# Layer 1's second pass with one matrix a channel and the pixels around the patches in pairs

## The chip, the cores and the metric

The kernel is one program on 1 core of a Trainium2 chip. The metric is the device time of one execution in microseconds (us). All arithmetic is in 32-bit floats. The core has TensorE (PE, matrix products out of the on-chip SBUF into the accumulators of PSUM), VectorE (DVE), ScalarE (ACT), GpSimd (POOL) and SyncE (SP), and 16 DMA engines that move data between HBM and SBUF. A transfer is begun by an instruction on SP, ACT or POOL.

## The reference

Four layers are applied, each with a residual, to `x` of 4 images x 48 channels x 256 x 256 pixels. The change is in layer 1, cut here to what matters:

```python
y = jnp.einsum('oc,bchw->bohw', w_in, x)              # 48 -> 288 channels
yp = y.reshape(B, C2, ht, P, wt, P).transpose(0, 1, 2, 4, 3, 5)
f = jnp.fft.rfft2(yp) * fft_mask[None]                 # in each 8 x 8 patch
yp = jnp.fft.irfft2(f, s=(P, P))
y = yp.transpose(0, 1, 2, 4, 3, 5).reshape(B, C2, H2, W2)
y = lax.conv_general_dilated(y, w_dw, ..., padding=((1, 1), (1, 1)), feature_group_count=C2)
x1, x2 = jnp.split(y, 2, axis=1)
g = jax.nn.gelu(x1, approximate=False) * x2            # 144 channels
return jnp.einsum('oc,bchw->bohw', w_out, g)
```

So for each of 288 channels: a filter within 8 x 8 patches, then a 3 x 3 convolution, which also needs pixels of the neighbouring patches; then the channels are multiplied in pairs.

## The kernel before

**Two streams.** `run` (L1210) emits two interleaved streams of work. Stream "a" runs layers 0 and 1 image by image, then layer 3 of all images; stream "b" runs the first statistics, `patch_weights`, and layer 2 of each image. Each generator yields a cost in a planner's units, and the stream whose clock is behind is advanced next (L1246). Afterwards a scheduler of the framework moves instructions on each engine by the times that it expects, except where `pinned` holds them. Layer 2 of image i is therefore executed beside layers 0 and 1 of image i+1; only image 0's layers 0 and 1 have no layer 2 beside them. `dma` (L213) begins transfers on SP for stream a and on POOL for stream b; layer 2's `look` (L890) begins its loads on ACT.

**Layer 1** has three stages for an image. The first pass (L616-636) makes the 288 channels and stores them to `hD` in HBM. The second pass (L637-715), which is what changes, applies filter, convolution and gate and stores to `gD`. The third stage (L716-770) projects back to 48 channels.

**Second pass.** A patch pair of 8 x 16 pixels is put on the 128 partitions, and the 512 patch pairs of the image are the columns. The 288 channels go in 72 groups (NG) of 4. For each group g, `fetch` (L678) begins four loads one group ahead: `hg` (1 MB, the pixels), `ct` (the filter, 128 x 128 a channel), `tt` (the nine taps as a 128 x 128 matrix from the pixels of the patch pair itself) and `ht` (the taps from the 52 pixels around it). Then for each channel

1. `filtered` (L652): a 128 x 128 matrix times 512 columns (L654), copied from PSUM to `ys`, by ACT for even channels (L660) and by DVE for odd ones (L658);
2. the rows of pixels around each patch pair are brought from `ys` to `yh` by 8 copies from SBUF to SBUF a group (L708-711): two of 16 rows, two of 8 rows, four of one row. They hold all four channels of the group, 2244 elements a row;
3. `gated` (L662), one group later (`todo`): the taps on the own pixels (L667, 128 rows) and on the pixels around (L668, 65 rows) are added up in one PSUM bank; for a pair of channels ACT applies gelu (L671) and DVE multiplies (L672) into `gt`. Every second group `gt` (1 MB) is stored to `gD` (L713).

That is 12 matrix products of 512 columns and 12 or 13 transfers a group. A 32-bit product is two instructions in the profile, so 1152 products are 2304 rows. Stream a has five PSUM banks.

**`patch_weights`** (L546) runs once, in stream b, beside layer 0 of image 0. A first loop over 72 groups makes the filter matrices by a product (L565) and stores them to `cD`; it yields 3 units a group. A second loop makes the tap matrices (L577) and stores them to `tD`; it yields 12 units for each of 15 blocks.

Of the kernel before, what the change touches and what calls it, by code (L numbers as in the profile page):

```python
# [8 lines left out]
F32 = mybir.dt.float32  # L9
I32 = mybir.dt.int32  # L10
AF = mybir.ActivationFunctionType
# [8 lines left out]
NS = 16  # L20
# [9 lines left out]
YW = 17  # L30
YC = 33 * YW
Y0 = YW + 1
YL = Y0 + 4 * YC + Y0


AROUND = [
# [2 lines left out]
]  # L39
NH = 52  # L40

NZ = 65

# [130 lines left out]
class Net:  # L176
# [369 lines left out]
    def patch_weights(self):  # L546


        nc, a = self.nc, self.a
        self.cD = self.dram.tile([NG, 128, 4, 128], F32, name="cD")[:]  # L550
        self.tD = self.dram.tile([4 * NG, (128 + NH) * 128], F32, name="tD")[:]
        with ExitStack() as ctx:
            w = ctx.enter_context(self.pool("pw", 1))
# [1 line left out]
            mask = self.filter_mask(a["L1_fft_mask"], [(0, 4 * NG)], w)  # L555
            dw = w.tile([9, 4 * NG], F32, name="dw")
            self.dma(dw[:], a["L1_w_dw"])
            for g in range(NG):
                m = sb.tile([128, 4, 128], F32, name="m", tag="m")
                for c in range(4):  # L560
                    nc.vector.tensor_scalar(
                        m[:, c, :], self.ri, mask[:, 4 * g + c : 4 * g + c + 1], None, ALU.mult
                    )
                ps = self.bank()
                nc.tensor.matmul(ps[:], self.ri, m[:].rearrange("p c k -> p (c k)"), start=True, stop=True)  # L565
                ct = sb.tile([128, 512], F32, name="ct", tag="ct")
                nc.scalar.copy(ct[:], ps[:])
                self.dma(self.cD[g].rearrange("p c k -> p (c k)"), ct[:])
                yield 3
            for q0 in range(0, (128 + NH) * 128, 4608):  # L570
                sh = sb.tile([9, 4608], F32, name="sh", tag="sh")
                self.dma(sh[:], a["c_shift"][:, q0 : q0 + 4608])
                for c0 in range(0, 4 * NG, 96):
                    tt = sb.tile([96, 4608], F32, name="tt", tag="tt")
                    for q in range(0, 4608, 512):
                        ps = self.bank()
                        nc.tensor.matmul(ps[:96, :], dw[:, c0 : c0 + 96], sh[:, q : q + 512], start=True, stop=True)  # L577
                        if q % 1024:
                            nc.vector.tensor_copy(tt[:, q : q + 512], ps[:96, :])
                        else:  # L580
                            nc.scalar.copy(tt[:, q : q + 512], ps[:96, :])
                    self.dma(self.tD[c0 : c0 + 96, q0 : q0 + 4608], tt[:])
                    yield 12

    def layer1(self, x, mr, y):
        nc, a = self.nc, self.a
# [50 lines left out]
        with ExitStack() as ctx:  # L637
            w = ctx.enter_context(self.pool("wb", 1))
            sb = ctx.enter_context(self.pool("bb", 2))
            ys = [w.tile([128, YL], F32, name=self.nm("ys")) for _ in range(2)]  # L640
            yhs = [w.tile([NZ, YL], F32, name=self.nm("yh")) for _ in range(2)]
            hts = [w.tile([NZ, 4, 128], F32, name=self.nm("ht")) for _ in range(3)]
            for t in ys + yhs + hts:
                nc.vector.memset(t[:], 0.0)

            pick = lambda t, k, c: t[:k, Y0 + YC * c : Y0 + YC * c + 32 * YW].rearrange(
                "p (h s b) -> p s h b", h=2, b=YW
            )[:, :, :, :16]
            order = lambda t: t.rearrange("p (s h b) -> p s h b", h=2, b=16)
            todo, gt = None, None  # L650

            def filtered(c):  # L652
                ps = self.bank()
                nc.tensor.matmul(  # L654
                    ps[:].rearrange("p (s n) -> p s n", n=32), ct[:, c, :], hg[:, :, c, :], start=True, stop=True
                )
                if c % 2:
                    nc.vector.tensor_copy(pick(yt, 128, c), order(ps[:]))  # L658
                else:
                    nc.scalar.copy(pick(yt, 128, c), order(ps[:]))  # L660

            def gated(c):  # L662
                go, yo, yho, to, ho = todo
                both = []
                for q in (c, c + 2):
                    ps = self.bank()
                    nc.tensor.matmul(order(ps[:]), to[:, q, :], pick(yo, 128, q), start=True, stop=False)  # L667
                    nc.tensor.matmul(order(ps[:]), ho[:, q, :], pick(yho, NZ, q), start=False, stop=True)  # L668
                    both.append(ps)
                gl = sb.tile([128, 512], F32, name="gl", tag="gl")  # L670
                nc.scalar.activation(gl[:], both[0][:], AF.Gelu)  # L671
                nc.vector.tensor_mul(  # L672
                    gt[:, :, 2 * (go % 2) + c, :], gl[:].rearrange("p (s n) -> p s n", n=32),
                    both[1][:].rearrange("p (s n) -> p s n", n=32),
                )


            def fetch(g):  # L678
                hg = sb.tile([128, NS, 4, 32], F32, name="hg", tag="hg")
                self.dma(hg[:].rearrange("p s c n -> p s (c n)"), hD[:, g])  # L680
                ct = sb.tile([128, 4, 128], F32, name="ct", tag="ct")
                self.dma(ct[:], self.cD[g])
                tt = sb.tile([128, 4, 128], F32, name="tt", tag="tt", bufs=3)
                ht = hts[g % 3]
                tv = self.tD[4 * g : 4 * g + 4].rearrange("c (k m) -> k c m", m=128)
                self.dma(tt[:], tv[:128])
                self.dma(ht[:NH], tv[128:])
                return hg, ct, tt, ht

            fetched = {0: fetch(0)}  # L690
            for g in range(NG + 1):
                if g < NG:
                    yt = ys[g % 2]
                    if g + 1 < NG:
                        fetched[g + 1] = fetch(g + 1)
                    hg, ct, tt, ht = fetched.pop(g)
                if todo is not None and todo[0] % 2 == 0:
                    gt = sb.tile([128, NS, 4, 32], F32, name="gt", tag="gt")
                for c in range(2):
                    if g < NG:  # L700
                        filtered(2 * c)
                        filtered(2 * c + 1)
                    if todo is not None:
                        gated(c)
                if g < NG:
                    yh = yhs[g % 2]
                    n = YL - 2 * Y0
                    for k, m, p0, dp, far in AROUND:  # L708
                        self.dma(
                            yh[k : k + m, Y0 : Y0 + n], yt[p0 : p0 + (m - 1) * dp + 1 : dp, Y0 + far : Y0 + far + n]  # L710
                        )
                if todo is not None and todo[0] % 2:
                    self.dma(gD[:, :, todo[0] // 2, :], gt[:].rearrange("p s c n -> p s (c n)"))  # L713
                todo = (g, yt, yh, tt, ht)
                yield 12
        st = self.stat.tile([CP, 129, 6], F32, name=self.nm("st"), tag="st" + self.stream, bufs=1)  # L716
        with ExitStack() as ctx:
# [586 lines left out]
```

## Time and profile before

| | us |
|---|---|
| runs (3): lowest, median, highest | 20766.17, 20775.92, 20789.14 |
| the profiled execution | 20767.55 |
| its span (first to last instruction) | 20765.8 |

| engine | busy us | share of the span |
|---|---|---|
| PE | 18830.0 | 91% |
| DVE | 10830.0 | 52% |
| POOL | 8656.1 | 42% |
| ACT | 5784.0 | 28% |

Where the second pass stands in the span, by the first and last start of its own-pixel products (L667):

| image | from us | to us | beside it |
|---|---|---|---|
| 0 | 2359.1 | 3240.5 | nothing of stream b |
| 1 | 6250.8 | 7393.6 | layer 2 of image 0 |
| 2 | 10412.9 | 11562.3 | layer 2 of image 1 |
| 3 | 14576.6 | 15720.9 | layer 2 of image 2 |

The costliest rows of the second pass, mean duration of one instruction (they overlap, so products that follow one another start closer together than this):

| row | count | busy us | mean ns |
|---|---|---|---|
| L654 PE `ps<-hg,ct` 128*128, 512 columns | 2304 | 1268.5 | 678 |
| L667 PE `ps<-ys,tt` 128*128, 512 columns | 2304 | 1183.1 | 635 |
| L668 PE `ps<-yh,ht` 65*128, 512 columns | 2304 | 1186.7 | 660 |
| L658 DVE COPY `ys<-ps` | 576 | 397.2 | 690 |
| L672 DVE `gt<-gl,ps` | 576 | 395.4 | 687 |
| L660 ACT COPY `ys<-ps` | 576 | 344.7 | 603 |
| L671 ACT ACTIVATE `gl<-ps` | 576 | 343.9 | 597 |

In a row, `128*128` are the rows and columns of the matrix that is held in PE, and `128x512 f32` the operand that streams through. The idle time beside a group and its releaser say what that engine waited for. A queue such as "SPq" is the engine's sequencer, which begins transfers.

### The profile page before, as it was taken

To read this page: it belongs to the slowest core of one execution; us is meant where nothing else is said; L and a number is where in the kernel's file an instruction comes from. 1 tells how busy PE (TensorE), PEld (TensorE's weight loads), DVE (VectorE), ACT (ScalarE), POOL (GpSimd) and SP (SyncE) were. 2 spreads that over 40 slices of the span, in tenths; PEclk is the share of its full clock that TensorE was granted. 3 is DMA by queue.
4 is the path that set the end of the run, shared out by engine and by line. 5 is a ranking of instruction groups with operands and counts; after the bars stand their busy time and mean duration, and the time that the engine had idled before them with its cause. 6 is when DMAs were issued, how large, how long until landed. Compare 5 with 4: busy or idle time off the path is not lost.

```text
span 20765.8 us, 232624 instructions
## 1 busy us (share of the span) xinstructions
PE 18830.0 (91%) x79032; PEld 11956.8 (58%) x79032; DVE 10830.0 (52%) x21947; ACT 5784.0 (28%) x12185; POOL 8656.1 (42%) x8899
## 2 busy tenths in 40 slices
PE   7998798999878889998788899987888999999999
PEld 4566335666543346665433466654334787878888
DVE  4544322477764544777645447776554255555511
ACT  2333312333331123333311233333112211111111
POOL 1000000177754511777545117775552066666600
PEclk9899799999968999999689999996888999999999
DMA  4623886555588975555889755558897566766633
GB/s 113 133 57 78 231 217 202 133 129 132 127 244 228 236 214 134 128 133 127 239 230 234 220 133 128 130 126 240 231 235 222 137 148 151 157 151 153 146 78 71
DMA packets 2494456, 3403.86 MB, mean 164 GB/s; under 512 B 595079, under 2 KB 2069631, under 8 KB 2382732
## 3 DMA queue, kind: packets, MB, share of 16 engines
q1 hardware_dynamic: 1906184, 2081.72, 38.4%
q0 software_dynamic: 452944, 1110.52, 21.5%
q10 hardware_dynamic: 134144, 196.73, 4.2%
q8 instruction: 635, 10.40, 0.2%
q14 instruction: 549, 4.49, 0.1%
HBM read 2450.46 MB, written 802.77 MB: 157 GB/s over the span
## 4 chain that ended last, share of the span: by engine, by line
PE 72%; DMA 14%; DVE 6%; POOL 4%; issue 2%; SPq 1%; ACT 1%; ACTq 0%; DVEq 0%; POOLq 0%
PE ps L353 22%; PE ps L361 5%; PE ps L876 5%; PE ps L654 4%; POOL V L974 3%; PE ps L668 3%; PE ps L667 3%; DMA ct<-cD 3%; PE ps L623 3%; PE ps L754 3%; PE ps L1120 2%; PE ps L901 2%; PE ps L811 2%; PE ps L505 2%; DMA A<-x 2%
## 5 line engine op out<-in xcount | busy, mean ns | idle before, releaser
L974 POOL DMA_INDIRECT V<-t,idx x8192 | 8240.8, 1006 | 4821.2 <-issue 2346.6
L353 PE MATMUL ps<-W,A 128*128 128x288 f32 (+1 forms) x24576 | 5566.1, 375 | 102.9 <-DMA A<-x 35.9
L353 PEld LDWEIGHTS ps<-W,A 128*128 128x128 f32 x24576 | 4295.0, 192 | 1252.3 <-issue 533.7
L214 POOL DMA_DIRECT2D X<-x x192 | 144.4, 756 | 4242.6 <-DMA x<-xt 3034.9
L987 DVE TENSOR_TENSOR V<-V 128x1536 f32<-128x1536 f32 (+3 forms) x2048 | 1845.3, 901 | 19.5
L985 DVE TENSOR_TENSOR V<-V,w 128x3072 f32<-128x3072 f32 x512 | 1713.6, 3347 | 33.2 <-DMA V<-t,idx 23.8
L654 PE MATMUL ps<-hg,ct 128*128 128x512 f32 x2304 | 1268.5, 678 | 394.7 <-DMA ct<-cD 275.0
L623 PE MATMUL ps<-win,xp 48*128 48x288 f32 x4096 | 1093.1, 622 | 515.8 <-DVE xp L610 237.6
L434 ACT COPY qkv<-ps 128x288 f32<-128x288 f32 x2048 | 763.7, 401 | 2681.8 <-PE ps L353 1180.0
L876 PE MATMUL ps<-A,W 128*96 128x512 f32 x3072 | 1483.5, 619 | 3.0 <-issue 3.0
L668 PE MATMUL ps<-yh,ht 65*128 65x512 f32 x2304 | 1186.7, 660 | 142.9 <-DMA yh<-ys 113.9
L361 PE MATMUL ps<-W,B 58*128 58x288 f32 (+1 forms) x8192 | 1271.0, 393 | 30.0 <-DMA B<-x 18.3
L457 DVE BATCH_NORM_STATS2 bs<-ps 128x6 f32<-128x96 f32 x2048 | 390.1, 252 | 1654.9 <-PE ps L455 1654.4
L1100 DVE TENSOR_TENSOR gp<-gl,ps 128x192 f32<-128x192 f32 x1024 | 354.4, 352 | 1716.6 <-ACT gl L1099 1706.0
L667 PE MATMUL ps<-ys,tt 128*128 128x512 f32 x2304 | 1183.1, 635 | 60.3 <-DVE ys L658 33.1
L623 PEld LDWEIGHTS ps<-win,xp 48*128 48x128 f32 x4096 | 686.5, 274 | 892.3 <-ACT hs L630 286.9
L654 PEld LDWEIGHTS ps<-hg,ct 128*128 128x128 f32 x2304 | 472.0, 212 | 1037.5 <-issue 928.6
L1099 ACT ACTIVATE gl<-ps 128x192 f32<-128x192 f32 x1024 | 331.3, 330 | 2619.7 <-PE ps L353 2318.5
L672 DVE TENSOR_TENSOR gt<-gl,ps 128x512 f32<-128x512 f32 x576 | 395.4, 687 | 1236.8 <-PE ps L668 1236.2
L361 PEld LDWEIGHTS ps<-W,B 58*128 58x128 f32 x8192 | 764.8, 187 | 452.1 <-issue 353.4
L876 PEld LDWEIGHTS ps<-A,W 128*96 128x96 f32 x3072 | 487.2, 168 | 853.4 <-issue 839.6
L658 DVE COPY ys<-ps 128x512 f32<-128x512 f32 x576 | 397.2, 690 | 1086.0 <-PE ps L654 897.3
(182 smaller groups left out, 24329.4 us busy)
## 6 DMA issues: line engine op xcount, KB each, us to landing
hD<-hs SPq DMA_DIRECT2D x64, 4608.0 KB
hg<-hD SPq DMA_DIRECT2D x288, 1024.0 KB
gD<-gt SPq DMA_DIRECT2D x144, 1024.0 KB
gs<-gD SPq DMA_DIRECT2D x64, 2304.0 KB
V<-t,idx POOLq DMA_INDIRECT x8192
A<-x SPq DMA_DIRECT2D x512, 193.5 KB
xt<-x SPq DMA_DIRECT2D x256, 387.0 KB
A<-x ACTq DMA_DIRECT2D x512, 193.5 KB
```

The source lines that it names most:

```text
L353: nc.tensor.matmul(to(q, b), A[:, r + q, 128 * b + g : 128 * b + g + 128], W[:, g, :], start=b == 0 and g == 0, stop=b == 1 and g == 2,)
L361: nc.tensor.matmul(to(q, b), B[p, r // 2, 128 * b : 128 * b + 128], W[p, 3, :], start=b == 1, stop=b == 0)
L434: nc.scalar.copy(t.qkv[:, 2 * q + b, :], banks[2 * b + q][:, 0:288])
L623: nc.tensor.matmul(ps[:, :288], xp[64 * h : 64 * h + 48, b, :], win[64 * h : 64 * h + 48], start=True, stop=True,)
L654: nc.tensor.matmul(ps[:].rearrange("p (s n) -> p s n", n=32), ct[:, c, :], hg[:, :, c, :], start=True, stop=True)
L667: nc.tensor.matmul(order(ps[:]), to[:, q, :], pick(yo, 128, q), start=True, stop=False)
L668: nc.tensor.matmul(order(ps[:]), ho[:, q, :], pick(yho, NZ, q), start=False, stop=True)
L754: nc.tensor.matmul(pp[:CP, :], pr[:, q, :], got[q][:], start=q == 0, stop=q == 2)
L876: m = nc.tensor.matmul(to[q], W[:, g, :], A[:, q:4:2, g : g + 256], start=q == 0 and g == 0, stop=q == 1 and g == 2,)
L974: nc.gpsimd.indirect_dma_start(out=V[:, k, 4 * cr : 4 * cr + 4, :].rearrange("p e c -> p (e c)"), out_offset=None, in_=table, in_offset=ba ...
L985: self.pinned(nc.vector.tensor_mul(Vm, Vm, wm.unsqueeze(2).to_broadcast([128, 64, 48])))
L987: nc.vector.tensor_add(V[:, :, 0:n, :], V[:, :, 0:n, :], V[:, :, n : 2 * n, :])
```

## The change

**Tables.** `cD` is replaced by `fD`, one block of 128 x 4 x 192 numbers a group. Its first 128 columns a channel are the product of the filter and the nine taps on the own pixels; its last 64 are the 52 columns of the filter that make the pixels around, already in the order of `yh` (the rest is zero). `patch_weights` makes the taps `tD` first and then, for each group, loads the own taps back, makes the filter as before, copies 52 of its columns in eight pieces, multiplies filter and taps in four products of 128 columns, copies the result and stores the block. It yields 5 units a group, not 3.

**Second pass.** `filtered` is gone. `around` makes only the rows around: for channels c and c+2 two products with 64-column matrices that write partitions 0-63 and 64-127 of one PSUM bank, and one ACT copy to `ye`. `gated` makes the own part straight from `hg` with the composed matrix, all four products first, then the four products on the pixels around, whose rows lie at 0-51 and 64-115. Each of the eight copies `ye` to `yh` is now made twice, for the two halves of the partitions, with two channels (1122 elements) a row: one begun on SP, one on ACT. `ht` is loaded in two transfers, `ct` and `tt` in one (`f`); loads go two groups ahead, with four buffers.

```diff
-YL = Y0 + 4 * YC + Y0
+YL = Y0 + 2 * YC + Y0
...
-NZ = 65
+NF = 128 + 64
...
-            for g in range(NG):
-                m = sb.tile([128, 4, 128], F32, name="m", tag="m")
...
-                self.dma(self.cD[g].rearrange("p c k -> p (c k)"), ct[:])
-                yield 3
...
+            fs = [w.tile([128, 4, NF], F32, name=self.nm("f")) for _ in range(2)]
+            for f in fs:
+                nc.vector.memset(f[:], 0.0)
+            for g in range(NG):
+                own = sb.tile([128, 4, 128], F32, name="own", tag="own")
+                self.dma(own[:], self.tD[4 * g : 4 * g + 4].rearrange("c (k m) -> k c m", m=128)[:128])
...
+                f = fs[g % 2]
+                for k, n, p0, dp, far in AROUND:
+                    nc.vector.tensor_copy(
+                        f[:, :, 128 + k : 128 + k + n], ct[:, :, p0 : p0 + (n - 1) * dp + 1 : dp]
+                    )
+                ps = self.bank()
+                for c in range(4):
+                    nc.tensor.matmul(
+                        ps[:, 128 * c : 128 * c + 128], ct[:, c, :], own[:, c, :], start=True, stop=True
+                    )
+                nc.scalar.copy(f[:, :, 0:128], ps[:].rearrange("p (c k) -> p c k", k=128))
+                self.dma(self.fD[g], f[:].rearrange("p c k -> p (c k)"))
+                yield 5
...
+            def around(c):
                 ps = self.bank()
+                for q in range(2):
+                    nc.tensor.matmul(
+                        strips(ps[64 * q : 64 * q + 64, :]), f[:, c + 2 * q, 128:NF], hg[:, :, c + 2 * q, :],
+                        start=True, stop=True,
+                    )
+                nc.scalar.copy(pick(ye, slice(0, 128), c), order(ps[:]))
+
+            def gated():
+                go, hgo, fo, yho, ho = todo
                 both = []
+                for c in range(2):
+                    both.append([self.bank() for _ in range(2)])
+                    for q in range(2):
+                        nc.tensor.matmul(
+                            strips(both[c][q][:]), fo[:, c + 2 * q, 0:128], hgo[:, :, c + 2 * q, :],
+                            start=True, stop=False,
+                        )
+                for c in range(2):
+                    for q in range(2):
+                        rows = slice(64 * q, 64 * q + NH)
+                        nc.tensor.matmul(
+                            order(both[c][q][:]), ho[rows, c, :], pick(yho, rows, c), start=False, stop=True
+                        )
...
             def fetch(g):
+                hg = sb.tile([128, NS, 4, 32], F32, name="hg", tag="hg", bufs=4)
                 self.dma(hg[:].rearrange("p s c n -> p s (c n)"), hD[:, g])
+                f = sb.tile([128, 4, NF], F32, name="f", tag="f", bufs=4)
+                self.dma(f[:].rearrange("p c k -> p (c k)"), self.fD[g])
+                ht = hts[g % 4]
+                for q in range(2):
+                    self.dma(
+                        ht[64 * q : 64 * q + NH],
+                        self.tD[4 * g + 2 * q : 4 * g + 2 * q + 2].rearrange("c (k m) -> k c m", m=128)[128:],
+                    )
+                return hg, f, ht
...
+            fetched = {0: fetch(0), 1: fetch(1)}
             for g in range(NG + 1):
                 if g < NG:
+                    ye, yh = yes[g % 2], yhs[g % 2]
+                    if g + 2 < NG:
+                        fetched[g + 2] = fetch(g + 2)
+                    hg, f, ht = fetched.pop(g)
+                    for c in range(2):
+                        around(c)
+                if todo is not None:
...
+                    gated()
                 if g < NG:
                     n = YL - 2 * Y0
                     for k, m, p0, dp, far in AROUND:
+                        for q, dma in ((0, self.dma), (64, nc.scalar.dma_start)):
+                            dma(yh[q + k : q + k + m, Y0 : Y0 + n], ye[q + k : q + k + m, Y0 + far : Y0 + far + n])
```

## The prediction

> **What bounds it now.** I read the page first, for where PE is not full, then busy time by stretch around the second pass, then who waited there for PE and for SP's queue, then the timeline of one group.
>
> ```profile
> PE   7998798999878889998788899987888999999999
> DMA  4623886555588975555889755558897566766633
> ```
> PE is near full except in four dips; DMA is high just there. The dips are layer 1. By stretch:
> ```profile
> 2346.00:3250.00 904.00, 829.91 (x1728) 345.24 (x1728) 207.98 (x296) 173.92 (x289) 0.00 (x0) 0.92 0.79 213
> 6234.00:7403.00 1169.00, 1016.95 (x2336) 430.23 (x2336) 605.14 (x892) 193.90 (x320) 612.06 (x639) 0.89 0.91 232
> ```
> (length, then busy PE, PEld, DVE, ACT, POOL; clock, DMA share, GB/s.) The second pass takes 904 us in image 0 and 1169 in image 1, 1180 and 1173 in images 2 and 3, PE busy 92% and 87%. From first to last start of L667 a group takes 881/71 = 12.4 us in image 0 and 1143/71 = 16.1 in image 1. PE isn't alone: the transfers are busy 91% there. SP's queue, image 1's stretch:
> ```profile
> SPq L214 <- DMA tt<-tD: 105.4, 46, 7.3
> SPq L214 <- DMA yh<-ys: 84.6, 70, 10.0
> SPq L214 <- DVE ys L658: 76.0, 40, 7.6
> SPq L214 <- DMA A<-x: 71.2, 20, 7.8
> ```
> (total us, times, longest.) SP issues for 660 us of this stretch, by the durations of its begins, and most of the rest it waits. It does not need `tt` or layer 2's `A` for anything. The instruction records say why it waits: every transfer begun by SP or ACT signals one of **eight semaphores**, in rotation over both queues, and its begin waits until the transfer eight places earlier has landed. So eight are in flight at most, and a late one stops whichever queue comes to its semaphore. One group:
> ```profile
> 2606.10 5.87 SPq L214 DMA_DIRECT2D yh<-ys  x8
> 2606.93 3.73 PE L668 MATMUL ps<-yh,ht 65*128 65x512 f32 x8
> 2610.49 1.88 PE L654 MATMUL ps<-hg,ct 128*128 128x512 f32 x4
> 2612.08 0.60 SPq L214 DMA_DIRECT2D gD<-gt  x1
> 2612.77 1.95 SPq L214 DMA_DIRECT2D hg<-hD  x1
> ```
> SP issues eight copies for 5.87 us, then a store, then the next loads: no gap. Eight rows of PE take 2610.49 - 2606.93 = 3.56 us, 0.445 each, so 24 rows a group are 10.7 us.
>
> **PE, parts removed.** Filter, own and around were 24 rows. The own part stays: 8 rows, 3.56 us. The pixels around now stand on 52 rows in two halves of the array. The trace has such pairs in layer 0:
> ```profile
> 1500.47 3.08 PE L353 MATMUL ps<-W,A 128*128 128x288 f32 x12
> 1503.47 1.24 PE L361 MATMUL ps<-W,B 58*128 58x288 f32 x8
> 1504.64 3.18 PE L353 MATMUL ps<-W,A 128*128 128x288 f32 x12
> ```
> 12 full rows take 3.00 us (0.25 each), 8 paired rows 1.17 (0.146): 0.585 of the price, switching included. So the halo costs 8 x 0.445 x 0.585 = 2.08 us. `around` pairs columns, not rows, which no row here shows: 2.08 if it pairs like L361, 3.56 if not at all. I take 2.08. Sum 7.7 us a group (9.2), 3.0 (1.5) less.
> The Trainium skill (TensorEngine Tiling (Array Packing), Tiling Modes) says that column tiles work independently, like row tiles; by it the lower price holds, and no run here shows it yet.
>
> **Other engines.** DVE loses two copies a group (0.690 each), ACT keeps two copies and two gelus (0.60 each). Both have room: DVE 605 of 1169.
>
> **Transfers, bytes.** From the packet records in image 0's stretch: `tt` 36864 packets of 512 B at 30 ns and `ct` 9216 of 2 KB at 86 go, 69 + 50 us over 16 engines; `f` is 9216 of 3 KB, at `ct`'s rate 129 ns, 74 us. The copies move the same bytes (3456 packets of 8976 B, 878 ns, become 6912 of half). Work 711 (0.787 x 904) - 45 = 666 us; in image 1, 1060 - 45 = 1015.
>
> **Transfers, begins.** This is the other side. SP has as many as before: 4 loads (two for `ht`), 8 copies, half a store: 650 us in image 0, 9.0 a group. ACT gets 8 copies, 2 x 0.59 + 2 x 0.61 + 4 x 0.73 = 5.3 us a group at SP's prices, in front of or between its copies and gelus. Through the eight semaphores go 20.5 transfers a group, not 12.5. Time from begin to landing, from the begins and the increments of the semaphores (fastest tenth and mean, image 0): `hg` 4.85 and 6.74; `ht` 5.87 and 7.68; an 8-row copy 4.29 and 6.81; a single row 2.33 and 4.18.
> The order is hg, f, ht, ht, then SP's and ACT's copies by turns. The third pair waits for `hg` and `f`, the fourth for the two `ht`, the eighth for the fourth. So from the begin of `hg`: `ht` begins at 1.4 (0.5 + 0.43 + 0.45) and lands at 7.3 to 9.1, the fourth copy then lands at 11.6 to 15.9, the eighth is issued (0.74), half a store (0.3): 12.6 to 16.9 us until the next `hg`. Half-sized packets save 0.4. Middle: 14.3. The same count for before (eighth copy waits for `ht`, nothing follows): 8.2 to 10.1, under PE's 10.7. **The rotation takes PE's place as the bound.** Image 0: 72 x (14.3 - 12.4) = +137.
> Image 1 (`ht` 6.24 and 8.71, 8-row 4.57 and 7.74): 13.2 to 18.9, middle 16.05 - 0.4 = 15.65, against 16.1 now. But SP's place in the rotation now depends on ACT's queue: layer 2's 154 ACT transfers a stretch (2.1 a group) cost SP 71.2/72 = 1.0 us a group; eight more cost between 0 and 8/2.1 x 1.0 = 3.8. I take the middle, 1.9: 17.55, 72 x 1.45 = +104 an image, +313 for three.
> Two loads in front do not help this: `hg` waited for its turn on SP, not for a buffer.
> The Trainium skill (DMA: Bandwidth & Descriptors, Rules for kernel authors) speaks against the split: two transfers to disjoint halves of the partitions share the same engines, one transfer is better; by it the copies gain nothing in bytes and pay twice the begins, as in my sum. Its page on SBUF (SBUF — State Buffer, Door 1) gives the halves different ports; if copies then ran at the 4608-byte gathers' 300 ns, 63 us less in image 0.
>
> **Tables.** `patch_weights` runs beside layer 0 of image 0, where PE is 97% busy (1570 of 1615 us), so its PE time is on the path. New: 8 rows of 128 columns a group. Lower price 0.153 (L811, 64 rows in 9.79 us), upper 0.25 (L353 with 288); I take 0.19, the length of a weight load: 72 x 8 x 0.19 = 109 us (88 to 144). Once it waits for the last `tD` to land, about 7. Its ACT copy (72 x 0.6), eight DVE pieces (72 x 8 x 0.17 = 98 us) and 0.4 MB more a group hide in engines under half busy there. The planner's 144 units more end long before layer 1 asks. +116.
>
> **Sum.** 20765.8 + 137 + 313 + 116 = 21,332; that execution took 20767.55 and the median is 20775.92, 8 us more, within the runs' own 23. I say **21,330**. Its own range, from the fast ends (12.2 us in image 0; 15.65 in the others; 95 for tables) to the slow ones, most of it: 20,950 to 21,700.
>
> **Rivals.**
> *Faster.* Small copies land early, the rotation never stops, and bytes bound the pass. For: 45 us less work, PE down by a quarter, no more waits of L654 for `ct`. Against: 20.5 x mean landing. Image 0 at 90% DMA share (what the others reach now): 666/0.90 = 740, -164; others halfway between 0.907 and 1: 1015/0.955 = 1063, -106 each. 20,766 - 164 - 318 + 116 = 20,400. Full shares (666 and 1015) would give 20,766 - 238 - 3 x 154 + 116 = 20,182. It decides if the fourth copy lands within about 9 us of `hg`'s begin.
> *Covered.* What PE gives back the rotation takes, both passes stay, only the tables are paid: 20,882.
> *ACT the bound.* The begins stand ahead of the gelus, which free PSUM; ACT's last copy goes at 17.3 us (second `ht` begins at 1.85 and lands at 9.5, the fourth copy lands at 16.5, plus 0.73): +353 in image 0; 15.65 + 3.8 = 19.4 in the others, +238 each: 21,950.
> *Not as said:* if column products don't pair, PE needs 9.2, still under 14.3: no change of the forecast.
>
> **How the numbers follow.** Forecast 0.45, covered 0.14, ACT 0.11, faster 0.27, cancelled 0.03. Under 0.2% (42 us) a measurement of this kernel can't tell from no change. Faster 0.27, same 0.03, slower 0.45 + 0.14 + 0.11 = 0.70. The range 20,400 to 21,750 leaves out half of the faster case and most of the ACT case, some 0.2.
>
> **What would show it.** Right: a group takes over 13 us in image 0, PE busy under 70% there, SP and ACT waiting on landings of `hg`, `ht` and `yh`, DMA share below 0.79. Wrong: DMA share near 0.95 in images 1 to 3 and PE waiting on nothing but `yh`. L577's successor should add some 110 us of PE before 1000 us.

## The result and the profile after

The change makes the kernel slower: median 21006.42 us of 4 runs (20998.45 to 21022.48) against 20776.27 of 4 before (20766.17 to 20789.14), ratio 1.0108 with a 95% interval of 1.0095 to 1.012. The profiled execution took 20998.45 us, its span is 20996.7, 230.9 longer. The stage boundaries of the two traces say where (second pass: first to last start of its products):

| stretch | before us | after us | difference |
|---|---|---|---|
| start of image 0's second pass (tables and layer 0 before it) | 2352.1 | 2401.8 | +49.7 |
| second pass, image 0 | 892.0 | 965.7 | +73.7 |
| second pass, image 1 | 1162.0 | 1184.9 | +22.9 |
| second pass, image 2 | 1163.5 | 1191.1 | +27.6 |
| second pass, image 3 | 1159.5 | 1186.1 | +26.6 |
| everything between and behind | | | +30.4 |

The page's rows of 40 slices, after:

```profile
PE   7999688999978889999788899997888899999999
...
DMA  4542766555587775555877755558787566667633
```

The four dips of PE have stayed, but the DMA row is lower in them (mostly 7, where it was 8 or 9). The stretches of the second pass in images 0 and 1 (length, then busy PE, PEld, DVE, ACT, POOL; clock, DMA share, GB/s):

```profile
2402.00:3352.00 950.00, 817.76 (x1696) 261.48 (x1694) 95.86 (x140) 169.74 (x284) 0.00 (x0) 0.82 0.65 188
6370.00:7537.00 1167.00, 1014.48 (x2302) 343.60 (x2300) 497.67 (x731) 186.81 (x315) 592.91 (x624) 0.82 0.80 220
```

Two things are seen. DVE lost its copies, DMA works less (0.65 of the stretch, it was 0.79), and nothing came of either. And PE is busy for 818 us in image 0, as long as in the 880 us before (817.25), though it was to have a quarter less to do: its clock is 0.82 (it was 0.92), and a product on the pixels around costs more than before, not half. Who waited, image 0 (total us, times, longest):

```profile
SPq L214 <- DMA f<-fD: 148.0, 68, 5.4
SPq L214 <- DMA yh<-ye: 127.8, 103, 3.7
...
SPq L214 <- DMA ht<-tD: 3.2, 5, 1.7
```
```profile
PE ps L696 <- DMA yh<-ye: 123.1, 34, 5.1
```

SP does not need `f`, nor any copy's landing: these are waits of the rotation, 279 us in some 70 groups, 3.9 us each. For `ye`, the data of its copies, SP hardly waited (under 3 us in the whole stretch; before the change it waited 62.7 us for `ys`). SP's begins are 8.8 us a group (5.53 for the copies, 3.27 for the rest), its waits for free buffers 0.4: 13.1 of a period of 13.4. PE in turn waits for the copies. The timeline of two groups (a number in brackets is PE's wait before the row, with what ended it):

```profile
2699.49 3.75 PE L696 MATMUL ps<-yh,ht 52*128 52x512 f32 x4 [2.64 <-DMA yh<-ye]
...
2705.82 5.87 ACTq L738 DMA_DIRECT2D yh<-ye  x8
...
2710.61 2.04 PE L696 MATMUL ps<-yh,ht 52*128 52x512 f32 x4
...
2712.45 1.94 SPq L214 DMA_DIRECT2D f<-fD  x1
2712.59 1.08 PE L677 MATMUL ps<-hg,f 128*64 128x512 f32 x4
...
2716.02 10.88 SPq L214 DMA_DIRECT2D yh<-ye  x8
...
2717.34 9.79 ACTq L738 DMA_DIRECT2D yh<-ye  x8
...
2728.19 3.75 PE L696 MATMUL ps<-yh,ht 52*128 52x512 f32 x4 [4.66 <-DMA yh<-ye]
```

`f`, begun at 2712.45, lands at 2722.3. SP's third copy, eight places behind it, stands until then, so that eight begins take 10.88 us where their own time is 5.5; ACT's take 9.79 in the same stretch, and 5.87 a group earlier, when nothing held them. PE finds `yh` only at 2728.19. Four rows of L677 take 1.08 us, 0.27 each: the column halves run side by side. Four rows of L696 take 2.04, 0.51 each: the row halves do not. The order of the instructions on PE is the likely reason, and e2 tests it: the two products of ACT's half (rows 64-115) were put first and the two of SP's half (rows 0-51), after which the gelus follow, behind the next group's `around`, so that neighbours always use the same rows.

### The profile page after: what moved, and what is told of

Read it like the earlier page. It is cut to its first block, busy times and chain, and to the rows that moved or that the text cites. A ratio compares the mean times of both kernels' runs of the same rounds, so it can differ in the third digit from the quotient of the medians.

```text
span 20996.7 us, 234381 instructions
## 1 busy us (share of the span) xinstructions
PE 18928.6 (90%) x79608; PEld 11701.3 (56%) x79608; DVE 10491.4 (50%) x21937; ACT 5810.4 (28%) x12257; POOL 8705.1 (41%) x8971
## 3 DMA queue, kind: packets, MB, share of 16 engines
q14 instruction: 550, 4.51, 0.1%
## 4 chain that ended last, share of the span: by engine, by line
PE 68%; DMA 16%; DVE 6%; POOL 4%; issue 3%; SPq 2%; ACT 1%; ACTq 1%; DVEq 0%; POOLq 0%
PE ps L353 22%; PE ps L361 5%; PE ps L903 4%; POOL V L1001 4%; PE ps L696 3%; PE ps L641 3%; DMA yh<-ye 3%; PE ps L781 3%; DMA f<-fD 2%; PE ps L689 2%; SPq L214 2%; PE ps L1147 2%; PE ps L928 2%; PE ps L677 2%; PE ps L505 2%
## 5 line engine op out<-in xcount | busy, mean ns | idle before, releaser
L696 PE MATMUL ps<-yh,ht 52*128 52x512 f32 x2304 | 1425.4, 747 | 347.6 <-DMA yh<-ye 317.1
L641 PE MATMUL ps<-win,xp 48*128 48x288 f32 x4096 | 1098.0, 626 | 519.2 <-DVE xp L628 230.6
L689 PE MATMUL ps<-hg,f 128*128 128x512 f32 x2304 | 1274.4, 697 | 214.9 <-ACT ye L681 209.1
L361 PE MATMUL ps<-W,B 58*128 58x288 f32 (+1 forms) x8192 | 1267.8, 392 | 22.1 <-DVE t L445 12.5
L696 PEld LDWEIGHTS ps<-yh,ht 52*128 52x128 f32 x2304 | 446.6, 217 | 1221.0 <-issue 844.0
L689 PEld LDWEIGHTS ps<-hg,f 128*128 128x128 f32 x2304 | 481.6, 224 | 1070.5 <-issue 592.0
L681 ACT COPY ye<-ps 128x512 f32<-128x512 f32 x576 | 338.4, 603 | 2293.3 <-DMA yh<-ye 1092.8
L677 PE MATMUL ps<-hg,f 128*64 128x512 f32 x2304 | 836.5, 769 | 149.8 <-DMA ht<-tD 107.4
```

Source lines behind the costliest of these rows:

```text
L361: nc.tensor.matmul(to(q, b), B[p, r // 2, 128 * b : 128 * b + 128], W[p, 3, :], start=b == 1, stop=b == 0)
L641: nc.tensor.matmul(ps[:, :288], xp[64 * h : 64 * h + 48, b, :], win[64 * h : 64 * h + 48], start=True, stop=True,)
L677: nc.tensor.matmul(strips(ps[64 * q : 64 * q + 64, :]), f[:, c + 2 * q, 128:NF], hg[:, :, c + 2 * q, :], start=True, stop=True,)
L689: nc.tensor.matmul(strips(both[c][q][:]), fo[:, c + 2 * q, 0:128], hgo[:, :, c + 2 * q, :], start=True, stop=False,)
L696: nc.tensor.matmul(order(both[c][q][:]), ho[rows, c, :], pick(yho, rows, c), start=False, stop=True)
```

## The experiments

The record names four chips, of two kinds. e1 to e4 ran on one like that of the result (before: 20,785 us). e5 to e8, e9 to e16 and e17 with e18 met three others, on which the kernel before takes 25,470 to 25,740 us: the stages after image 0 are longer there in every kernel, so that absolute times of the two kinds must not be set against each other. Image 0's second pass is nearly the same on both (the changed kernel: 965.7 us in the trace of the result and 954.5 in that of e14, the same kernel run again on a slower chip as the control), and serves as the common measure. "Image 0" below is that pass, first to last start of its products, in one trace a run. Runs of one kernel differ in it by up to 6 us, those two by 11. The passes of images 1 to 3 are compared within one kind only; the control's take 1369 to 1382 us.

**e1, the corner copies left out.**

```diff
-                    for k, m, p0, dp, far in AROUND:
+                    for k, m, p0, dp, far in AROUND[:4]:
```

> The changed kernel without the eight copies of one row a group (four corners, two halves): rows 48-51 and 112-115 of yh stay zero, so the corner pixels are left out of the result. 12.5 transfers a group go through the eight semaphores, as before the change, not 20.5. Theory (the rotation of eight sets the pass): image 0's second pass falls from 950 us to 830-870 (PE's own 818 us and a few waits), images 1 to 3 from 1170 to 1050-1110; total 21,006 - 100 - 3 x 90 = about 20,640 (20,500 to 20,750). Rival (PE's products are the bound, 818 us busy and the granted clock of 0.82 stays): the pass loses at most the waits that the corner copies cause directly, under 20 us an image: 20,930 or more.

Measured: 20359.33 us, ratio to before 0.9798 (0.9782 to 0.9814); image 0 817.7, the others 1022, 1021 and 1025. More than the theory said (20,500 to 20,750): 8 of 20.5 transfers cost some 640 us. The run takes away begins, rotation places and bytes at once and does not tell them apart. SP's begins fell from 8.7 to 5.9 us a group, its waits in the rotation did not fall (279 us in the changed kernel, 341 here), and PE was busy for 93% of the pass, as it is in the kernel before.

**e2, the halves side by side.**

```diff
-                        nc.tensor.matmul(
+                        self.pinned(nc.tensor.matmul(
                             order(both[c][q][:]), ho[rows, c, :], pick(yho, rows, c), start=False, stop=True
-                        )
+                        ))
```

> The changed kernel with the four products of the pixels around held in the program's order, so that the products on rows 0-51 and 64-115 stand side by side. Now they stand apart and take 0.60 us of PE each from start to start. Rival (PE is the bound, and the halves that were put apart cost the expected gain): the products on the pixels around fall from 337 us to about 180 in image 0, the pass from 950 to 800-830, others by as much: 21,006 - 4 x 130 = about 20,490. Theory (the rotation is the bound): PE is busy for less, by 100 to 150 us an image, but waits that much longer; the time stays within 80 us of 21,006, and could be longer, since the first pair now waits for SP's copies, which land last.

Measured: 20897.76 us, 1.0056 (1.0039 to 1.0073); image 0 942.2. PE's timeline in e2:

```profile
2711.43 1.08 PE L677 MATMUL ps<-hg,f 128*64 128x512 f32 x4
2712.63 2.14 PE L696 MATMUL ps<-yh,ht 52*128 52x512 f32 x8
2716.57 1.08 PE L677 MATMUL ps<-hg,f 128*64 128x512 f32 x4 [1.79 <-ACT ye L681]
```

Eight rows now take 2.14 us (the forecast's 2.08). PE spends 208 us on them, it was 344, and its idle time grows from 132 to 279 us: of 136 us saved 23 arrive. PE is not the bound. (The total fell by 109 us, where the theory had allowed 80.)

**e3, all copies on SP.**

```diff
-                        for q, dma in ((0, self.dma), (64, nc.scalar.dma_start)):
+                        for q, dma in ((0, self.dma), (64, self.dma)):
```

> The changed kernel with all 16 copies of a group begun on SP. As many transfers in the rotation, and 14.3 us of begins a group on one queue. Theory (the rotation is the bound, whichever queue begins): a little slower, since the begins no longer overlap: image 0's group 13.2 to 14.5-15.5, total 21,050 to 21,500. Rival (ACT's begins in front of its copies and gelus are what costs): faster, ACT's copies come 6 to 10 us earlier: 20,700 to 20,900.

Measured: 21980.41 us, 1.0577 (1.0559 to 1.0595); image 0 1248.2. SP's begins alone are 14.1 us a group of 17.3. So ACT's part of the begins is worth far more than it costs; the rival falls, and the theory had the size wrong (14.5 to 15.5).

**e4, ACT's half of the copies on POOL.**

```diff
-                        for q, dma in ((0, self.dma), (64, nc.scalar.dma_start)):
+                        for q, dma in ((0, self.dma), (64, nc.gpsimd.dma_start)):
```

> The changed kernel with the half of the copies that ACT begins moved to POOL, whose transfers count on semaphores of their own. SP and ACT have 12.5 transfers a group in their rotation. In image 0 POOL has nothing else. Theory (the rotation is the bound): image 0's second pass from 950 to 830-880; images 1 to 3 can go either way, since POOL's queue also carries layer 2's gathers there (POOL is busy 593 of 1167 us): 1100 to 1250. Total 20,650 to 21,200, and image 0 is what decides. Rival (PE is the bound): image 0 stays at 930 to 950.

Measured: 21134.72 us, 1.0164 (1.0147 to 1.0181); image 0 843.2, the others 1276, 1273 and 1266. Image 0's stretch, and PE's waits in image 1's:

```profile
2407.00:3234.00 827.00, 764.20 (x1692) 245.91 (x1692) 95.16 (x139) 170.17 (x283) 281.46 (x568) 0.88 0.74 216
```
```profile
PE ps L696 <- DMA yh<-ye: 123.1, 34, 14.5
PE ps L696 <- DMA V<-t,idx: 75.5, 12, 13.6
```

With the same copies and the same bytes, but 12.5 transfers in the rotation, image 0 falls by 122 us; PE, its halves still apart, is busy for 781 of the 843. SP's own begins did not get fewer (8.7 us a group, now 9.1), its waits in the rotation fell from some 280 to 127 us. So this gain is not one of SP's begins; ACT, though, lost its eight begins a group to POOL. In image 1 the copies stand behind layer 2's gathers (`V`).

**e5, the loads on POOL.**

```diff
-                self.dma(hg[:].rearrange("p s c n -> p s (c n)"), hD[:, g])
+                nc.gpsimd.dma_start(hg[:].rearrange("p s c n -> p s (c n)"), hD[:, g])
...
```

> The changed kernel with the four loads of a group (hg, f, ht twice) begun by POOL, on semaphores of its own, in place of SP; 16.5 transfers a group stay in the rotation of SP and ACT, all of the copies' begins stay where they are. Theory (slow landings in the rotation stop the copies that come eight places later; f's alone stopped SP 137 us in image 0): image 0's second pass from 966 to 840-900. In images 1 to 3 the loads stand behind layer 2's gathers on POOL, as the copies did in e4: 1190 to 1290. Rival (it is the number of copies and their begins, not what the loads do in the rotation): image 0 stays above 930.

Measured: 25028.41 us, 0.9819 (0.9784 to 0.9855); image 0 930.6, the others 1236, 1230 and 1203. SP's waits in image 0:

```profile
SPq L214 <- DMA yh<-ye: 310.9, 251, 4.9
SPq L214 <- ACT ye L681: 111.0, 69, 8.3
```

Image 0 gains 24 us on the control, no more than e2 did, and the scheduler had put the halves side by side here too. In image 0 it is thus not the slow loads that fill the rotation, and the theory's 840 to 900 was missed: without the loads the 16 copies wait for one another. Beside layer 2 it is different. There the passes are 130 to 170 us shorter than the control's, and this is where the total's gain comes from; which wait it was that went was not tried.

**e6, e9, e16, the split alone, in the kernel before.**

```diff
-                        self.dma(
-                            yh[k : k + m, Y0 : Y0 + n], yt[p0 : p0 + (m - 1) * dp + 1 : dp, Y0 + far : Y0 + far + n]
-                        )
+                        for o, dma in ((0, self.dma), (n // 2, nc.scalar.dma_start)):
+                            at = Y0 + o
+                            dma(
+                                yh[k : k + m, at : at + n // 2],
+                                yt[p0 : p0 + (m - 1) * dp + 1 : dp, at + far : at + far + n // 2],
+                            )
```

> The kernel before the change with nothing changed but its eight copies a group: each is made in two, channels 0-1 begun on SP and channels 2-3 on ACT. Same matrices, same products, same bytes; 20.5 transfers a group, not 12.5, and eight begins on ACT in front of its copies and gelus. Theory (the split is what costs): image 0's second pass from 892 to 950-1030, the others from 1162 to 1190-1270, total 20,785 + 80 + 3 x 60 = about 21,050 (20,900 to 21,300). Rival (the loss comes from the new matrices, the halves that PE takes apart and the clock): 20,785 within 60.

> e6 once more (the kernel before, each copy split in two, half of them on ACT), because e6 to e8 met a chip on which the kernel before itself takes 25,469 us. Theory (the split alone costs): on a chip like the first, 21,050 to 21,500, image 0's second pass 950 to 1100 for 892. Rival (it cost only there): 20,785 within 60.

> e6 and e9 once more (the kernel before with its copies split in two, half begun by ACT), for its time on a chip like the first: image 0's second pass 1220 for 892, the others 1300 to 1450 for 1162, total 21,600 to 22,200. Rival (the loss of 3% came from the slower chip alone): under 21,300.

Measured: 26251.4, 26503.9 and 26439.58 us, ratios 1.0313 (1.0272 to 1.0354), 1.0316 (1.0289 to 1.0342) and 1.0294 (1.0275 to 1.0314); image 0 1220.8, 1224.3 and 1221.4 for 892.0. All three met slower chips, so the totals expected of the first stay untried; image 0 lost more than e6 and e9 had expected. Waits in image 0 of e16:

```profile
SPq L214 <- DMA yh<-ys: 579.0, 197, 7.5
```
```profile
ACT ys L660 <- PE ps L654: 555.5, 123, 27.1
ACT gl L671 <- DMA yh<-ys: 401.8, 66, 6.7
```

The split by itself costs 329 us in image 0. SP waits 579 us for copies eight places earlier, and since loads go one group ahead here, PE waits 258.8 us for `ct`. The rest of the change, with less work for PE and deeper loads, gives some 255 of these 329 us back.

**e7, e10, loads one group ahead.**

```diff
-            fetched = {0: fetch(0), 1: fetch(1)}
+            fetched = {0: fetch(0)}
...
-                    if g + 2 < NG:
-                        fetched[g + 2] = fetch(g + 2)
+                    if g + 1 < NG:
+                        fetched[g + 1] = fetch(g + 1)
```

> The changed kernel with its loads one group ahead, not two. Theory: the loads' depth bought nothing, since what waits is the copies: 21,006 within 80 us. Rival (two groups of loads in front stand in the rotation ahead of the copies, and this is the loss): 20,850 or less. A third case: the loads were needed that early, PE waits for hg and f: 21,100 or more.

> e7 once more (the changed kernel with loads one group ahead). Theory: two groups ahead bought nothing: 21,006 within 80 us. The runs of e7 point to the third case (PE waited for f 227 us in image 0): 21,080 to 21,300.

Measured: 25785.9 and 25967.96 us, 1.0128 (1.0089 to 1.0168) and 1.0108 (1.0073 to 1.0143), where the changed kernel itself stands at 0.9984 (e14, on the chip of e10); image 0 1095.1 and 1098.0 for 954.5. PE's waits in e10:

```profile
PE ps L677 <- DMA f<-fD: 302.1, 64, 8.3
```

The third case: the second group in front is worth 140 us in image 0. The theory, that depth buys nothing, was wrong: when the rotation delays the loads, only depth hides that.

**e8, e11, whole copies.** The rows around are put 4 (8, 64) apart, so that one constant step of partitions serves both halves; the tap and filter columns are ordered alike.

```diff
-    (0, 16, 112, 1, -YW), (16, 16, 0, 1, YW), (32, 8, 15, 16, -1), (40, 8, 0, 16, 1),
+    (0, 4, 16, 112, 1, -YW), (1, 4, 16, 0, 1, YW), (2, 8, 8, 15, 16, -1), (6, 8, 8, 0, 16, 1),
...
-NH = 52
+NH = 64
...
-                        for q, dma in ((0, self.dma), (64, nc.scalar.dma_start)):
-                            dma(yh[q + k : q + k + m, Y0 : Y0 + n], ye[q + k : q + k + m, Y0 + far : Y0 + far + n])
+                        rows = slice(k, k + (2 * m - 1) * step + 1, step)
+                        self.dma(yh[rows, Y0 : Y0 + n], ye[rows, Y0 + far : Y0 + far + n])
```

> The changed kernel with eight copies a group that serve both halves of the partitions at once, all on SP: the rows around are put at a constant distance (up 0, 4, 8.., down 1, 5, 9.., left 2, 10.., right 6, 14.., corners 3, 19, 35, 51, and the same 64 further on), so that one stride runs through both halves; the matrices hold 64 rows for 52, with zeros. All of the result is computed. 12.5 transfers a group, as before the change and as in e1, with the whole of the copied data; both halves' products wait for the same copies and stand side by side. Theory (number of transfers and begins): like e1 or below it, image 0's second pass 770 to 830, the others 980 to 1060; total 20,250 to 20,450. Rival (what e1 saved was the corners' own data or PE's wait for them): 20,700 or more.

> e8 once more (eight copies a group at one stride through both halves, all on SP; 12.5 transfers). Theory (number of transfers and begins): image 0's second pass 740 to 800, the others 980 to 1060, total 20,150 to 20,400. Rival (bytes set it again): images 1 to 3 at 1060 to 1100, total 20,400 to 20,550.

Measured: 24837.37 and 25052.99 us, 0.9741 (0.9705 to 0.9778) and 0.9744 (0.9722 to 0.9766); image 0 746.9 and 741.4. The other passes take 1191 to 1247 us, for the control's 1369 to 1382. All pixels are copied, so what e1 saved was not the corners' data: the number of transfers is what costs. The Trainium skill (DMA: Bandwidth & Descriptors, Rules for kernel authors) has the rule for it, one transfer in place of two on disjoint partition halves. The trace agrees: whole copies take 213 us off image 0 (741.4 for the control's 954.5). SP's waits in e11:

```profile
SPq L214 <- DMA hg<-hD: 62.6, 38, 2.5
SPq L214 <- DMA f<-fD: 61.0, 69, 2.1
```

SP's account says where the 213 us, 3.0 a group, went. Its waits in the rotation fell from 277 us in the control's stretch to 128 here, 2.1 a group; its begins from 8.6 to 7.7 us a group; its waits for free buffers grew by 0.4. The packets of the copies got shorter as well (376 ns in the changed kernel, 211 here, means), but a copy did not land sooner: after 5.7 us with 32 rows and 4.9 with 16, where SP's halves of 16 and 8 rows had taken 4.5 and 2.9. How much is due to the products that stand side by side here, as in e2, was not tried apart.

**e12, e15, the taps in `f`'s block.** On top of e11: `fD` has 256 more columns, `patch_weights` loads the taps into them, and `ht` is no load of its own.

```diff
-        self.fD = self.dram.tile([NG, 128, 4 * NF], F32, name="fD")[:]
+        self.fD = self.dram.tile([NG, 128, 4 * NF + 256], F32, name="fD")[:]
...
-                for q in range(2):
-                    self.dma(
-                        ht[64 * q : 64 * q + NH],
-                        self.tD[4 * g + 2 * q : 4 * g + 2 * q + 2].rearrange("c (k m) -> k c m", m=128)[128:],
-                    )
-                return hg, f, ht
+                return hg, f, ft[:, 4 * NF :].rearrange("p (c m) -> p c m", m=128)
```

> e11 with the two loads of ht taken into f's: patch_weights puts the 64 rows of taps behind the composed matrices in fD, and a group loads hg and f alone, 10.5 transfers. Theory (landings of slow loads in the rotation): 30 to 60 us an image less than e11, 20,000 to 20,250. Rival (with 12.5 the rotation no longer binds, bytes or PE do): within 40 us of e11.

> e12 once more, for its time on a chip like the first: image 0's second pass 680 to 700; the others, where layer 2 stands beside, 960 to 1050; total 19,950 to 20,300, faster than the kernel before by 2.3 to 4%.

Measured: 24931.88 and 24894.89 us, 0.9703 (0.9676 to 0.973) and 0.9692 (0.9672 to 0.9711); image 0 689.4 and 690.8, some 50 less than e11, as expected. In e15 the stretch reads:

```profile
2413.00:3085.00 672.00, 576.11 (x1680) 190.97 (x1680) 94.76 (x138) 169.32 (x281) 0.00 (x0) 0.94 0.80 267
```

This is the fastest version, 3% under both kernels on this chip; on one of the first kind it was not run.

**e13, e14, e17: PE and ACT relieved.** e13 moves the copies of `ye` from ACT to DVE; e14 is the changed kernel; e17 is e13 with e2's edit.

```diff
-                nc.scalar.copy(pick(ye, slice(0, 128), c), order(ps[:]))
+                nc.vector.tensor_copy(pick(ye, slice(0, 128), c), order(ps[:]))
```

> The changed kernel with the two copies from PSUM to ye on DVE in place of ACT; every transfer, its queue and its place in the rotation stay. In the changed kernel ACT's queue is one closed chain: eight begins 7.62 us from first to last (their own 6.07), a copy, two gelus and a copy of 0.6 each, and 3.4 us of waits for PE between them, 13.4 in all, which is the period. Theory (this chain on ACT sets the period, and the copies and waits behind the begins are part of it): a period of 10.7 to 12.0 us, image 0's second pass 780 to 880, total 20,400 to 20,700 on the first chip. Rival (the rotation of eight alone sets it): nothing changes in it, image 0 stays above 940 and the total within 100 of 21,006.

> The changed kernel as it is, beside the others on the same chip. A chip like the first: 21,006 within 40. A chip on which the kernel before takes 25,500: unknown in absolute terms; by ratio 1.00 to 1.03, image 0's second pass 950 to 980 on either.

> e2 and e13 together: the products of the pixels around held in the program's order, so that the halves stand side by side, and the copies to ye on DVE. Alone they took 23 us (e2) and 20 us (e13) off image 0's second pass. Theory (two chains of nearly one length: PE with its halves apart, 11.4 us a group and waits, and ACT with begins, copies and gelus, 13.1 to 13.4; whichever one is shortened, the other stays): together they take far more than the sum, image 0 at 760 to 860. Rival (the rotation of eight sets it, whatever PE and ACT do): the sum at most, 910 to 930.

Measured: e13 25650.91 us, 0.9976 (0.996 to 0.9991), image 0 934.6; e14 25624.48, 0.9984 (0.9968 to 0.9999), image 0 954.5; e17 25602.87, 0.9939 (0.9923 to 0.9956), image 0 936.3. e17's stretch and SP's waits in it:

```profile
2405.00:3323.00 918.00, 644.21 (x1692) 215.67 (x1692) 187.37 (x282) 81.21 (x140) 0.00 (x0) 0.83 0.67 195
```
```profile
SPq L214 <- DMA yh<-ye: 98.3, 80, 4.0
SPq L214 <- DMA hg<-hD: 78.1, 58, 3.3
SPq L214 <- DMA ht<-tD: 74.5, 65, 2.4
```

The theory of two chains falls: PE is busy for 644 us, ACT for 81, and the pass stays at 936. What does not change is SP: 8.6 us of begins a group, 3.55 of waits in the rotation (250.9 us over some 70 groups) and 0.7 for buffers make 12.9 of a period of 13.0. e13's range (780 to 880) was missed by the same theory.

**e18, hg and f begun by ACT in e15.**

```diff
-                self.dma(hg[:].rearrange("p s c n -> p s (c n)"), hD[:, g])
+                nc.scalar.dma_start(hg[:].rearrange("p s c n -> p s (c n)"), hD[:, g])
...
-                self.dma(ft[:], self.fD[g])
+                nc.scalar.dma_start(ft[:], self.fD[g])
```

> e15 (eight whole copies on SP, the taps in f's block) with hg and f begun by ACT, which has 5.5 us a group free there; 10.5 transfers in the rotation as before. In e15 SP begins or waits for nearly all of its period of 9.66 us (copies 7.15 from first to last, the others 2.07). Theory (SP's begins are what is left in image 0): 689 to 630-670; with layer 2 beside nothing much, total 24,895 - 40 to 150 on the slower chip. Rival (bytes or PE, 8.2 us a group, set it): within 15 us in image 0; ACT's begins in front of gelus may cost up to 60.

Measured: 25076.91 us, 0.9734 (0.9716 to 0.9752); image 0 758.4, 68 longer than e15. PE's and SP's waits:

```profile
PE ps L701 <- DMA yh<-ye: 152.3, 35, 7.7
```
```profile
SPq L214 <- DMA yh<-ye: 113.2, 51, 4.9
SPq L214 <- DMA f<-fD: 60.4, 31, 5.3
```

SP has two begins a group less to make and the pass is longer: its copies now wait in the rotation for loads that ACT begins when its own queue gets to them. Begins on SP are thus not the whole of it; the order across two queues that share eight places has a price of its own.

## Why the prediction was right and wrong

**Direction and mechanism** held: 20.5 transfers through eight places in place of 12.5 took PE's place as the bound, and the DMA share fell below 0.79 (to 0.65). A group took 13.4 us, over the 13 that was named as a sign. e1, e4, e11 and e15 show the number of transfers as the lever; e2, e13 and e17 exclude PE's products and ACT's copies. ACT's eight begins, 6.1 us a group, were taken away only together with places in the rotation (e1, e4, e11). Of SP's 13 us a group 8.8 are begins and 3.9 waits in the rotation; what either would save alone stays open, since the number of semaphores was not changed.

**The size** was wrong: +554 to 566 forecast, +231 measured. The terms of the sum that were mis-sized, in the order of what they cost:

*Images 1 to 3, +104 each, measured +23 to +28.* The group went from 16.1 to 16.45 us, so that of the forecast's 1.45 us of loss 0.35 arrived. The step that failed is the 15.65, and in it "Half-sized packets save 0.4": the 8-row copy was taken to land 4.57 to 7.74 us after its begin less that 0.4, and landed after 3.48 on SP, in the mean. Against it stands that SP's begins other than the copies' took 3.2 us a group, where some 2.1 had been counted. The other term, "I take the middle, 1.9", for ACT's begins in SP's rotation, came out: sorted by who had begun the transfer eight places earlier, SP's waits in image 1's stretch hold 153 us for copies begun by ACT, 2.1 a group. That leaves some 14.3 for the rest.

*Image 0, +137, measured +74.* "Half-sized packets save 0.4" is the step. Taken were landings of the 8-row copy of 4.29 to 6.81 us less that 0.4. The halved copies land far sooner:

| from begin to landing, image 0, mean us | before | after, SP | after, ACT |
|---|---|---|---|
| copy of 16 rows | 6.99 | 4.51 | 3.46 |
| copy of 8 rows | 6.79 | 2.91 | 2.80 |
| copy of one row | 4.18 | 2.23 | 3.48 |
| `ht` | 7.45 | 5.77 | |

(The forecast had 7.68 for `ht` before; counted again it is 7.45. The copies' packets took 376 ns; the sum had half of 878, the more hopeful case 300.) Against it stand three things: the other begins on SP took 3.27 us a group, where 0.5 + 0.43 + 2 x 0.45 + 0.3 had been counted; `f`, whose landing the sum left out, lands after 7.04 and holds SP for 148 us; and all of SP's 127.8 us of waits for copies were for copies begun by ACT, 1.8 a group, a term that the sum has for images 1 to 3 and not for image 0. The errors partly cancel: 13.4 us a group for 14.3.

*Tables, +116, measured +50.* The step is "I take 0.19, the length of a weight load". From start to start the 576 new products take 66.4 us, 0.115 each, below the lower price of 0.153. A nearer row was there: layer 0's transposes with 128 columns (L493), in the same stretch, after the change of one duration with them (groups of PE by line: busy us, mean ns of one; first after, then before):

```profile
L596 PE MATMUL ps<-own,ct 128*128 128x128 f32 x576 | 78.1, 279 | 0.0
...
L493 PE MATMUL ps<-c_ident_sb,un 128*96 128x128 f32 x140 | 23.1, 277 | 0.0
```
```profile
L493 PE MATMUL ps<-c_ident_sb,un 128*96 128x128 f32 x140 | 23.4, 295 | 0.0
```

These start 0.117 us apart in the trace before, over the whole of layer 0. Of the 66, 17 came back: up to the second pass the other products took 10.6 us less and PE idled 6.1 less.

*The stages between and behind the passes,* +30 in the table above, had no term in the sum; what made them longer was not looked into.

*PE, 7.7 us a group,* was wrong in one term and in the clock, though that cost little: `around` pairs as assumed, the products on the pixels around do not (0.60 from start to start in the mean), and PE was busy 86%, not under 70%. e2 shows that the 2.08 was right for a pair that stands together, and that nobody was waiting for it.

*"Two loads in front do not help this"* was wrong by 140 us in image 0 (e10): its reason, that `hg` waits for its turn on SP and not for a buffer, holds, but a load that gets its turn late is hidden by the group that it is ahead.

**The rivals.** ACT as the bound gave the wrong size (21,950), and without its copies on ACT the pass fell by no more than 20 us (e13). Covered (20,882) would have been nearest in number, with passes unchanged; they were not. Faster had the condition that the fourth copy lands within about 9 us of `hg`'s begin; in image 0 SP's fourth landed after 11.5 in the mean.

## What to carry to other kernels

Count the transfers that share one ring of semaphores, and their begins on each queue, before the bytes: here 16 half copies for 8 whole ones cost more than the products saved were worth, and one constant step of partitions made them 8 again. Where a stage is bound by a queue, a shorter engine only waits longer; undo parts until the period moves. Take a price from the row with the same number of streamed columns, and look at the order that the scheduler made before counting on neighbours.

## What was not expected of the hardware

**A wait of PE costs more than its length.** In the timeline above four rows of L696 take 3.75 us after a wait of 4.66, and 2.04 when nothing stood before them. Some 7 us after that wait the products still start 0.85 us apart, then 0.43. The granted clock shows it: 0.50 from 2726 to 2736 us, then 1.00. Over image 0's pass it was 0.92 before, with 17 waits over 1.5 us, and 0.82 after, with 36. The Trainium skill (TensorE: Matmul & The Clock Gate, Why this matters for your kernels) warns of gaps over about 3 us between bursts of products. In these traces shorter ones go with it as well: the wait of 2.64 us above stands beside 10 us at 0.50 too, and before the change 22 of the pass's 27 stretches at half clock stand beside waits under 3 us.

**Row halves overlap only as neighbours.** Same products, same rows: 0.51 us each when neighbours use the same half, 0.27 when the halves alternate (e2).

**Chips differ by 24%** for the same kernel (20,785 and 25,685 us), and not evenly. Up to the end of image 0 the traces agree (the second pass starts at 2401.8 and 2406.0 us). Afterwards they part: from 4400 to 6500 us of e14, beside layer 2's gathers, PE waits for 504 us, 270 of them for nothing that the profile shows; from 4000 to 5800 us of the first it waits for 70, none of that kind. On the chip of e14 the change itself makes no difference to speak of (0.9984). What differs there was not tried.
